# A third Strassen level inside one product of seven, with its PSUM bank held over three steps

## The chip, the cores and the metric

The kernel runs on one core of a Trainium2 chip. The metric is the device time of one launch in microseconds (us). Three timed runs of the kernel before gave 819.54, 820.01 and 820.28 us; the median is 820.01 us.

## The reference, cut to what matters

All data are fp32. `x` has 4 x 1024 tokens of 1024 features.

```
xn = layernorm(x)
g  = sigmoid(xn @ gate_w.T + gate_b);   u_g = xn * g          # gate product
s  = recurrence over tokens of b * u_g ... + d_eff * u_g      # y of the recurrent branch
h  = silu(xn @ w1.T)                                          # product "u"
h  = silu(h @ w3.T)                                           # product "m"
h  = h @ w2.T
out[expert of token] += gate of token * h                     # 8 rows receive anything (top 2 of 8)
result = x + s * silu(out)
```

Only eight rows of the routed sum are not zero, so the kernel sums the 4096 rows of `h` into eight by their gates first and multiplies by `w2` afterwards, and of the recurrence and of the gate product it computes only what these eight rows and the mean over tokens need. What is left as heavy work is the product with `w1` (called u), that with `w3` (called m), both for all 4096 tokens, and the gate product (called g) for 1024 of them.

## The kernel before

**Tiling.** The tokens are taken in four blocks of 1024, `sb` = 0 to 3. They are called groups 0 to 3 in the name of the change; here they are called blocks, because "group" is needed for something smaller. In each block the 1024x1024x1024 product u, and then m, is computed by two levels of Strassen's algorithm in Winograd's form. The outer level replaces eight 512-wide products by seven, here called groups, with the indices 1 to 7. The order in which they run is written in the dictionary `order` (L205): 1, 2, 5, 6, 7, 4, 3 for u and 1, 5, 6, 2, 7, 4, 3 for m. The inner level replaces the eight 256-wide products of a group by seven, here called small products. `small` (L869) issues one: four matmuls of 128x128 weights with 256 moving columns, which sum into one PSUM bank of 128x512. An operand of a group is a `block` (128x4x512, four quadrants of 128x512), and a sum of quadrants is a `quarter` (128x512). There are 20 blocks and 18 quarters (L125), both handed out in a ring: `Held` (L111) pops the one that was dropped longest ago.

**One group.** `Half.step(n)` (L919) runs the seven small products of a group, n = 0 to 6, into three banks: X for n = 0, 2, 4, 6; Z for n = 1, 5; Y for n = 3. X and Z come from pools of two banks, Y from a pool of one (L104 to 106). After each product VectorE (DVE) adds the bank to a quadrant of the result: `first` for the first product that reaches a quadrant, `more` for a later one. Where there is nothing to add yet (groups 1 and 5), `first` is a copy by ScalarE (ACT). `whole` (L1005) follows when a quadrant is complete: in groups 6 and 7 it is one more DVE addition of two blocks for each quadrant, and in the groups that finish a block of results it calls `done`, where ACT applies the SiLU in place. The product of n = 3 is the one that the change replaces:

```python
            elif n == 3:
                Y = ps_y.tile([P, 2 * Q], F32, tag="Y", name=f"Y_{self.tag}")
                go(Y, A[:, 1], t[:, 2], True, True)
                ...
                    self.more(0, Y)
```

**Order.** Every engine runs its instructions in the order in which the program is written (`Pinned`, L79). That order is made by places. One place is the time of one small product; a group starts seven places after the one before it, and its step n stands at place S + 2n, S being its start. So the steps of two neighbouring groups alternate: between step 3 of one group at S + 6 and step 4 at S + 8 lies step 0 of the next group at S + 7. Everything else is put at a place with `at` (L186), and is issued by `run_todo` ahead of the step that stands there. A generator gives up its turn with `yield`, and goes on that many places later.

**What stands around the steps.** `left_sums` (L846) makes the four sums of token quadrants of a group on GpSimd (POOL), from place S - 6 on. The sums of weight quadrants are made in block 0 (`fresh_sums`, L546), stored in HBM, and loaded again in blocks 1 to 3 by the queue of SyncE (SP): `load_kept` and `load_kept_sum` (L629, L635). `s1` to `s4` (L785 to L844) make the four sums of token blocks of the outer level, on POOL for u of blocks 1 to 3 and on DVE elsewhere. `norm` (L407) normalises the tokens of the next block on DVE during m. `route` (L439) finds the experts of a block early in its u: TensorE computes the logits, DVE finds the two largest and their indices, ACT takes the sigmoids of their difference, and DVE builds the gates (tiles `lg`, `mx`, `ix`, `df`, `oh`, `C`). `scatter` (L1060) sums the finished rows of a block into eight.

Of the kernel before, what the change touches and what calls it, by code (L numbers as in the profile page):

```python
# [10 lines left out]
F32 = mybir.dt.float32  # L11
# [3 lines left out]
ALU = mybir.AluOpType  # L15
AX = mybir.AxisListType
P = 128
Q = 256
# [4 lines left out]
def kernel(  # L23
# [49 lines left out]
    NS = NTOK // SB  # L73
# [5 lines left out]
    class Pinned:  # L79
# [15 lines left out]
    nc = tc.nc  # L95
    pe, dve, act, pool, sync = (
        Pinned(e) for e in (nc.tensor, nc.vector, nc.scalar, nc.gpsimd, nc.sync)
    )
# [7 lines left out]
    ps_y = ctx.enter_context(tc.tile_pool(name="ps_y", bufs=1, space=bass.MemoryType.PSUM))  # L106
# [15 lines left out]
            if self.uses == 0:  # L122
                self.home.append(self.tile)

    NB, NQ = 20, 18  # L125
    IDLE = 13
    blocks = deque(
        const.tile([P, 4, 2 * Q], F32, tag=f"b{i}", name=f"b{i}") for i in range(NB)
# [8 lines left out]
    def quarter(uses=1):  # L137
        return Held(quarters, uses)
# [47 lines left out]
    def at(place, f, *args):  # L186

        seq[0] += 1
        heapq.heappush(todo, (place, seq[0], f, args))
# [8 lines left out]
    def resume(p, g):  # L198
        step = next(g, None)
        if step is not None:  # L200
            at(p + step, resume, p + step, g)
# [14 lines left out]
    start = {}  # L216
# [301 lines left out]
    kept = {}  # L518
    op_t = {}
# [14 lines left out]
    def keep_quarter(name, i, j, o):  # L534
        d = dramp.tile([P, 2 * Q], F32, tag=f"{name}_{i}_{j}", name=f"{name}_{i}_{j}")
        sync.dma_start(d, o.tile)
        kept[name, i, j] = d
        o.drop()
# [177 lines left out]
    def first_w3():  # L716
# [48 lines left out]
    S_OF = {  # L765
        1: (0, 0),
        2: (0, 1),
        4: (1, 1),
        5: "s1",
        6: "s2",  # L770
        3: "s4",
        7: "s3",
    }
    left = {}
# [91 lines left out]
                yield 2 * (A_AT[j + 1] - A_AT[j])  # L866


    def small(ps, A, B, start, stop, rows_first):  # L869

        for mt in range(2):
            for kt in range(2):
                w, m = (A, B) if rows_first else (B, A)
                pe.matmul(
                    ps[:, mt * Q : (mt + 1) * Q],
                    w[:, kt * Q + mt * P : kt * Q + (mt + 1) * P],
                    m[:, kt * Q : (kt + 1) * Q],
                    start=(start and mt == 0 and kt == 0),
                    stop=(stop and mt == 1 and kt == 1),
                    skip_group_check=True,  # L880
                )
# [3 lines left out]
    class Half:  # L885
# [30 lines left out]
        def whole(self, q):  # L916
            whole(self.kind, self.sb, self.i, q)

        def step(self, n):  # L919
            if n == 0:  # L920
                self.begin()
            A, t = self.A, self.t
            ts = [op_ts.get((self.kind, self.sb, self.i, j)) for j in range(4)]
            s = [left_q.get((self.src, self.sb, self.i, j)) for j in range(4)]

            def go(ps, a, b, start, stop):
                small(ps, a, b, start, stop, self.rows_first)

            if self.plain:

                q = ((0, 1, 2, 3) if self.i == 1 else (0, 3, 1, 2))[n // 2]
                ps = self.X if n // 2 % 2 == 0 else self.Z
                go(ps, A[:, q // 2 * 2 + n % 2], t[:, n % 2 * 2 + q % 2], n % 2 == 0, n % 2 == 1)
                if n % 2:
                    self.first(q, ps)
            elif n == 0:
                go(self.X, A[:, 0], t[:, 0], True, False)
                self.first(0, self.X)
            elif n == 1:
                go(self.Z, s[0].tile, ts[0].tile, True, False)  # L940
                self.first(3, self.Z)
                s[0].drop()
                ts[0].drop()
            elif n == 2:
                go(self.X, s[1].tile, ts[1].tile, False, False)
                self.first(1, self.X)
                s[1].drop()
                ts[1].drop()
            elif n == 3:
                Y = ps_y.tile([P, 2 * Q], F32, tag="Y", name=f"Y_{self.tag}")  # L950
                go(Y, A[:, 1], t[:, 2], True, True)
                if (self.kind, self.i) == ("g", 1):
                    at(Y_AT, self.more, 0, Y)
                else:
                    self.more(0, Y)
            elif n == 4:
                go(self.X, s[2].tile, ts[2].tile, False, False)
                self.more(3, self.X)
                s[2].drop()
                ts[2].drop()  # L960
            elif n == 5:
                go(self.Z, s[3].tile, t[:, 3], False, True)
                self.more(1, self.Z)
                s[3].drop()
            elif n == 6:
                go(self.X, A[:, 3], ts[3].tile, False, True)
                self.first(2, self.X)
                self.whole(2)
                ts[3].drop()
            if n == (7 if self.plain else 6):  # L970
                self.A.drop()
                t.drop()
# [265 lines left out]
    for kind, sb, i, plain in line:  # L1238
        h = Half(kind, sb, i, plain)
        halves.append(h)  # L1240
        S = start[kind, sb, i]
        n = 2 if sb == 0 and kind == "u" and i not in PLAIN_G else 1
        if kind != "g" and not plain:
            at(S + 2 - 8, left_sums, kind, sb, i, n)
        if kind != "g" and sb > 0:
            at(S - 10, load_kept, kind, sb, i)
            for j in range(4):
                at(S + 2 * T_AT[j] - 9, load_kept_sum, kind, sb, i, j)

    for sb in range(NS):  # L1250
        n = 2 if sb == 0 else 1
# [252 lines left out]
```

## Time and profile before

| | us |
|---|---|
| median of three timed runs | 820.01 |
| span of the profiled execution, first to last instruction | 817.9 |
| PE (TensorE matmul) busy | 810.6, 99% of the span |
| PEld (weight loads) busy | 696.5 |
| DVE busy | 509.7 |
| POOL busy | 496.1 |
| ACT busy | 263.8 |

The page gives no other time for the profiled execution than its span; the median of the timed runs lies 2.1 us above it. A row of the profile names the line, the engine, the operation, "out<-in" by the names of the tiles without their numbers, the shapes and the count. One fp32 matmul shows as two records on PE and two weight loads on PEld, so a small product is eight records. All work goes through the helper at L89, so rows are told apart by the names of the tiles. In the rows of the timeline the columns are the start, the time from the first start to the last end, the engine and its work, and, in brackets, how long the engine stood idle before it and who ended that. The ends of matmuls are modelled: a record of 0.38 us overlaps the next one, which starts 0.216 us after it.

By stretches of the span, u of blocks 1, 2 and 3 runs at about 290 to 375, 460 to 545 and 630 to 712 us, and m of block 3 from 712 to the end. POOL is busy for 52.6 us of the 85 us from 290 to 375.

### The profile page before, as it was taken

How to read it: one execution, taken by the hardware profiler on the slowest of the kernel's cores; microseconds unless marked ns; L12 is line 12 of the kernel's file. 1: busy time of each engine (PE TensorE's matmuls, PEld its weight loads, DVE VectorE, ACT ScalarE, POOL GpSimd, SP SyncE). 2: the span in 40 equal slices, each digit the busy share in tenths (PEclk: the TensorE clock that was granted, in tenths of full speed). 3: DMA queues.
4: the chain of work that ended last, by engine and by line, in shares of the span. 5: the costliest groups of instructions: out<-in, count | busy, mean ns of one | idle time of the engine just before them, and what ended most of it. 6: DMA issues, size and time to landing. Idle time of an engine off the chain costs nothing.

```text
span 817.9 us, 11299 instructions
## 1 busy us (share of the span) xinstructions
PE 810.6 (99%) x4085; PEld 696.5 (85%) x4085; DVE 509.7 (62%) x868; ACT 263.8 (32%) x458; POOL 496.1 (61%) x398
## 2 busy tenths in 40 slices
PE   8999999999999999999999999999999999999997
PEld 7888888888888878888888788888888788888885
DVE  6886598765588524764985235666983246667643
ACT  1245126877232237341022065421122021220111
POOL 2799896967999394744547453755448454465300
PEclk9999999999999999999999999999999999999999
DMA  9946619465978947629955875559666365555700
GB/s 338 421 175 232 230 47 357 171 246 160 411 267 309 345 174 293 241 103 385 376 179 210 332 279 190 187 206 426 242 244 257 104 219 203 196 180 195 283 14 2
DMA packets 55927, 192.88 MB, mean 236 GB/s; under 512 B 6480, under 2 KB 9792, under 8 KB 44224
## 3 DMA queue, kind: packets, MB, share of 16 engines
q1 hardware_dynamic: 55552, 191.61, 63.5%
q8 instruction: 33, 0.54, 0.3%
q10 hardware_dynamic: 320, 0.54, 0.2%
q14 instruction: 22, 0.18, 0.1%
HBM read 169.01 MB, written 39.87 MB: 255 GB/s over the span
## 4 chain that ended last, share of the span: by engine, by line
PE 98%; DMA 1%; DVE 0%; ACT 0%; issue 0%; SPq 0%
PE X_u L89 24%; PE X_m L89 24%; PE Z_u L89 12%; PE Z_m L89 12%; PE X_g L89 6%; PE Y_m L89 6%; PE Y_u L89 6%; PE Z_g L89 3%; PE acc L89 2%; PE plT L89 2%; PE Y_g L89 1%; DMA b<-in_x 1%; PE pp L89 0%; DVE bn L89 0%; PE accB L89 0%; PE ta L89 0%
## 5 line engine op out<-in xcount | busy, mean ns | idle before, releaser
L89 POOL TENSOR_TENSOR q<-b 128x512 f32<-128x512 f32 x154 | 203.0, 1331 | 193.7 <-PE X_m L89 48.0
L89 ACT ACTIVATE b<-b 128x512 f32<-128x512 f32 (+1 forms) x152 | 105.3, 696 | 298.1 <-DVE b L89 291.6
L89 POOL TENSOR_TENSOR q<-b,q 128x512 f32<-128x512 f32 x98 | 133.1, 1361 | 7.2 <-issue 4.0
L89 POOL TENSOR_TENSOR b<-b,b 128x512 f32<-128x512 f32 x72 | 92.9, 1310 | 48.5 <-PE X_u L89 33.7
L89 DVE TENSOR_TENSOR b<-b,b 128x512 f32<-128x512 f32 x120 | 109.2, 925 | 2.7
L89 PE MATMUL X_m<-q,q 128*128 128x256 f32 x448 | 105.9, 379 | 0.0
L89 PE MATMUL X_u<-q,q 128*128 128x256 f32 x432 | 102.4, 380 | 0.0
L89 DVE TENSOR_TENSOR b<-X_u,b 128x512 f32<-128x512 f32 x87 | 60.0, 690 | 57.8 <-PE X_u L89 57.1
L89 DVE TENSOR_TENSOR b<-X_m,b 128x512 f32<-128x512 f32 x88 | 60.4, 688 | 56.9 <-PE X_m L89 56.7
L89 PEld LDWEIGHTS X_m<-q,q 128*128 128x128 f32 x448 | 85.0, 190 | 12.4 <-issue 0.8
L89 POOL TENSOR_TENSOR q<-q,b 128x512 f32<-128x512 f32 x56 | 73.6, 1314 | 32.4 <-PE X_u L89 25.1
L89 PEld LDWEIGHTS X_u<-q,q 128*128 128x128 f32 x432 | 81.8, 190 | 12.2 <-issue 1.2
L89 DVE TENSOR_TENSOR b<-b,bc 128x1024 f32<-128x1024 f32 x56 | 67.8, 1211 | 0.1
L89 PE MATMUL X_u<-b,b 128*128 128x256 f32 x248 | 58.4, 380 | 0.0
L89 PE MATMUL Y_m<-b,b 128*128 128x256 f32 x224 | 53.1, 380 | 0.0
L89 PE MATMUL Z_m<-b,q 128*128 128x256 f32 x224 | 53.0, 380 | 0.0
L89 PE MATMUL X_m<-b,b 128*128 128x256 f32 x224 | 53.0, 379 | 0.0
L89 PE MATMUL Z_m<-q,q 128*128 128x256 f32 x224 | 52.9, 379 | 0.0
L89 PE MATMUL X_m<-q,b 128*128 128x256 f32 x224 | 52.9, 379 | 0.0
L89 PEld LDWEIGHTS X_u<-b,b 128*128 128x128 f32 x248 | 47.0, 190 | 6.7 <-DVE b L89 0.4
L89 DVE TENSOR_TENSOR b<-Z_u,b 128x512 f32<-128x512 f32 x47 | 32.4, 690 | 31.6 <-PE Z_u L89 30.7
L89 PE MATMUL Z_u<-q,q 128*128 128x256 f32 x216 | 51.1, 380 | 0.0
(182 smaller groups left out, 1171.6 us busy)
## 6 DMA issues: line engine op xcount, KB each, us to landing
q<-w SPq DMA_DIRECT2D x168, 256.0 KB, 4.5
b<-in_w SPq DMA_DIRECT2D x36, 1024.0 KB, 9.0
b<-w_T SPq DMA_DIRECT2D x24, 1024.0 KB, 6.3
b<-in_xT SPq DMA_DIRECT2D x15, 1024.0 KB, 12.9
w<-q SPq DMA_DIRECT2D x56, 256.0 KB, 7.4
b<-in_x SPq DMA_DIRECT2D x12, 1024.0 KB, 11.0
w_T<-b SPq DMA_DIRECT2D x8, 1024.0 KB, 4.4
b<-in_gw SPq DMA_DIRECT2D x6, 1024.0 KB, 14.0
```

The source lines that it names most:

```text
L89: r = f(*args, **kwargs)
```

## The change

In u of blocks 1 to 3 and in m of block 3, 28 groups in all, the small product of step 3 is computed by a third level of Strassen's algorithm: seven products of 128x128x128, each one matmul with 128 moving columns, in place of eight (that is, of four matmuls with 256). All go into bank Y of the group, which is now taken at the first of three steps:

- `eighth(0)` at place S + 1: two matmuls, and two DVE additions of 128x128 from the bank to the result;
- `eighth(1)` at place S + 3.6: one matmul and one such addition, of a quarter of the bank that is summed on;
- `eighth(2)` in step 3 at S + 6: four matmuls, one DVE addition of the whole bank (128x512), and one of 128x128.

The operands of the third level are sums of quarters of a quadrant. `token_thirds` makes three on POOL for each of the 28 groups at S - 2; `weight_thirds` makes four on POOL at S - 3, for u of block 1 and m of block 3; in u of block 1 they are stored in HBM, and `load_thirds` loads them at S - 3 in u of blocks 2 and 3. The ring of quarters grows from 18 to 24, and the argument `dynamic_dma_scratch_size=1024` makes room for it.

```diff
-    NB, NQ = 20, 18
+    NB, NQ = 20, 24
...
+    def is_third(kind, sb, i):
+        return sb > 0 and kind == "u" or (kind, sb) == ("m", NS - 1)
+    def cut(t):
+        return t.rearrange("p (k n) -> p k n", n=P)
+    def token_thirds(kind, sb, i):
+        a = cut(left[kind, sb, S_OF[i]][:, 1])
+        t = quarter()
+        o = cut(t.tile)
+        third_s[kind, sb, i] = t
+        pool.tensor_tensor(
+            o[:, 0:2], a[:, 1:2].to_broadcast([P, 2, P]), a[:, 0::3], ALU.subtract
+        )
+        yield 1
+        pool.tensor_tensor(o[:, 2], a[:, 0], o[:, 1], ALU.subtract)
+        pool.tensor_tensor(o[:, 3], a[:, 2], o[:, 2], ALU.subtract)
+    def weight_thirds(kind, sb, i):
...
+        pool.tensor_tensor(o[:, 1], b[:, 1], b[:, 0], ALU.subtract)
+        yield 1
+        pool.tensor_tensor(o[:, 2], b[:, 3], o[:, 1], ALU.add)
+        pool.tensor_tensor(o[:, 3], b[:, 2], o[:, 2], ALU.subtract)
+        yield 1
+        pool.tensor_tensor(o[:, 0], b[:, 1], b[:, 3], ALU.add)
+        yield 1
+        if again:
+            keep_quarter(name, i, "t", t)
+    def load_thirds(kind, sb, i):
+        o = quarter()
+        sync.dma_start(o.tile, kept[{"u": "w1", "m": "w3"}[kind], i, "t"])
+        third_t[kind, sb, i] = o
...
+        def eighth(self, n):
...
+            d = cut(self.dst[:, 0])
+            z, w = (1, 2) if self.rows_first else (2, 1)
+            if n == 0:
+                self.Y = ps_y.tile([P, 2 * Q], F32, tag="Y", name=f"Y_{self.tag}")
+            ps = cut(self.Y)
...
+            if n == 0:
+                go(3, a[:, 0], b[:, 0], True, False)
+                go(z, S[:, 1], T[:, 1], False, False)
+                add(d[:, 0], ps[:, 3])
+                add(d[:, 3], ps[:, z])
+            elif n == 1:
+                go(3, S[:, 2], T[:, 2], False, False)
+                add(d[:, z], ps[:, 3])
+            else:
+                go(z, S[:, 3], b[:, 3], False, False)
+                go(w, a[:, 3], T[:, 3], False, False)
+                go(0, a[:, 2], b[:, 2], False, False)
+                go(3, S[:, 0], T[:, 0], False, True)
+                add(self.dst[:, 0], self.Y)
+                add(d[:, w], ps[:, 3])
+                third_s[key].drop()
+                third_t[key].drop()
+                self.whole(0)
...
+            elif n == 3 and is_third(self.kind, self.sb, self.i):
+                self.eighth(2)
...
+        if is_third(kind, sb, i):
+            for n, step in enumerate((1, 3.6)):
+                at(S + step, h.eighth, n)
+            at(S - 2, token_thirds, kind, sb, i)
+            fresh = sb == 1 or kind == "m"
+            at(S - 3, weight_thirds if fresh else load_thirds, kind, sb, i)
```

## Prediction

> **What bounds the kernel now.** I read the page first: the busy time by engine and the chain that ended last.
>
> ```profile
> PE 810.6 (99%) x4085; PEld 696.5 (85%) x4085; DVE 509.7 (62%) x868; ACT 263.8 (32%) x458; POOL 496.1 (61%) x398
> ...
> PE 98%; DMA 1%; DVE 0%; ACT 0%; issue 0%; SPq 0%
> ```
>
> PE is busy all the time and carries the chain; in the waits by engine PE has none after 9 us of more than 0.3 us. So PE time that is taken away is gained, if no wait takes its place. Both sides need short times, so I went on to the timeline: what a record with 128 columns costs, and how long PE's banks take to come back.
>
> ```profile
> 8.75 0.83 PE L89 MATMUL idle<-ident,ones 128*128 128x128 f32 x6
> ...
> 805.20 0.60 PE L89 MATMUL tT<-ident,b 128*128 128x128 f32 x4
> 805.64 1.89 PE L89 MATMUL X_m<-q,b 128*128 128x256 f32 x8
> ```
>
> In a row of n records the spacing is (time - one record)/(n - 1). With 256 columns it is (1.89 - 0.38)/7 = 0.216 us. With 128 columns and full weights it is (0.83 - 0.276)/5 = 0.111 in `idle` and (0.60 - 0.272)/3 = 0.109 in the transposes `tT`, which have other weights each time. I take `idle`, which is a true fp32 matmul of two records.
>
> **The gain.** A small product is 8 x 0.216 = 1.73 us now, and 14 x 0.111 = 1.55 in three pieces of 0.44, 0.22 and 0.89. That is 0.17 us for each of 28, or 4.9 us (5.7 by `tT`, 2.1 by the 0.118 of `ta`, which is bound by its loads).
>
> A rule speaks against that. The Trainium skill, "TensorE: Matmul & The Clock Gate", Part 3, "The mechanism", says that a weight load overlaps a running matmul only where the two use different row groups. By it a record would wait for its own load, at least 0.109 more by `ta`, and the change would cost 28 x (14 x 0.22 - 1.73) = 38 us. The 0.111 of `idle` with a load for each record does not agree with it, and I go by the row.
>
> **The price: less cover for the banks.** Now every bank is followed by whole products of 1.73 us before PE needs it, or its neighbour, again. These rows show how long a bank takes to come back.
>
> ```profile
> 34.53 0.65 DVE L89 TENSOR_TENSOR b<-X_g,b 128x512 f32<-128x512 f32 x1
> 35.23 0.94 PEld L89 LDWEIGHTS X_g<-b,q 128*128 128x128 f32 x5 [0.35 <-DVE b L89]
> 35.23 1.13 PE L89 MATMUL X_g<-b,q 128*128 128x256 f32 x4
> ```
>
> DVE ends at 35.18 and PE goes on 0.05 later. The load isn't hidden then: the first record takes 0.48 in place of 0.38, so 0.10 more. In front of it, DVE starts 0.20 us after the next product's first record (X_u below: Y_u's first at 485.17, the addition at 485.37), because the last record drains. An addition takes 0.69, or 0.72 if the next one needs its result (756.37 - 755.65 on DVE); a 128x128 one I put at 0.29, from 0.42 for 256 and 0.69 for 512 columns.
>
> *Bank X.* Step 0 of the next group, at S + 7, takes the bank that the group before read out after its step 6, at S + 5. What lies between is step 3, now 0.89 instead of 1.73. The bank needs 0.20 + 0.69 + 0.05 + 0.10 = 1.05 (1.04 unrounded): 0.16 late. Where ACT copies (groups 1 and 5: 0.19 + 0.585 + 0.15 = 0.93) it is 0.04. In each of four stretches of seven groups it is five of the first kind and two of the second: 20 x 0.16 + 8 x 0.04 = 3.5 us. Bounds: 0, if release and load are quicker by 0.16, and 4.5.
>
> *Bank Y.* It is one bank only. So far seven places lie between two uses; now `eighth(2)` ends at S + 7 and the next group's `eighth(0)` stands at S + 8, one product later. It needs 0.20 + 0.72 + 0.29 + 0.05 + 0.10 = 1.36, and has 0.16 (from X) + 1.73 = 1.89. So an ordinary group costs nothing, but every delay on DVE over 0.5 us stops PE. I looked for such delays.
>
> First, `route`:
>
> ```profile
> 485.17 1.89 PE L89 MATMUL Y_u<-b,b 128*128 128x256 f32 x8
> 486.90 1.89 PE L89 MATMUL X_u<-b,b 128*128 128x256 f32 x8
> ...
> 485.37 0.69 DVE L89 TENSOR_TENSOR b<-X_u,b 128x512 f32<-128x512 f32 x1 [0.50 <-PE X_u L89]
> 488.46 0.23 DVE L89 TENSOR_TENSOR oh<-pl,ix 128x64 f32<-128x64 f32 x1 [2.40 <-ACT pl L89]
> 488.60 0.68 DVE L89 TENSOR_TENSOR b<-Y_u,b 128x512 f32<-128x512 f32 x1
> ...
> 486.09 0.63 ACT L89 ACTIVATE b<-b 128x512 f32<-128x512 f32 x1 [0.91 <-DVE b L89]
> 486.74 1.28 ACT L89 ACT_TABLE_LOAD   x1
> 488.04 0.39 ACT L89 ACTIVATE pl<-df 128x8 f32<-128x8 f32 x2
> ```
>
> DVE's `oh` waits 2.40 us for ACT, which has a SiLU and a 1.28 us table load ahead of the sigmoids. The addition of Y_u queues behind `oh` and starts at 488.60, 1.54 after Y_u has ended. Today nobody waits for that. In the changed program the order on DVE is the same: X_u, `oh`, then the two additions of `eighth(2)`; the next group's first matmul in Y waits for them. All of ACT's chain starts with the X_u addition at 485.37, which does not move. PE then reaches that matmul at 485.17 + 0.89 + 0.16 + 1.73 = 487.95; the bank is there at 488.60 + 0.72 + 0.29 + 0.15 = 489.76. That is 1.8 us, and `oh` waits the same 2.40 in all three blocks: 5.4 us (bounds 4 and 6.6, by 0.4 us to either side).
>
> Second, the extra additions of `whole`, and `s1` and `s4` of the last m:
>
> ```profile
> 509.54 0.69 DVE L89 TENSOR_TENSOR b<-X_u,b 128x512 f32<-128x512 f32 x1 [1.03 <-PE X_u L89]
> 510.34 1.06 DVE L89 TENSOR_TENSOR b<-b,b 128x512 f32<-128x512 f32 x1
> 511.32 0.68 DVE L89 TENSOR_TENSOR b<-Y_u,b 128x512 f32<-128x512 f32 x1
> ...
> 711.14 1.28 DVE L89 TENSOR_TENSOR b<-b,b 128x512 f32<-128x512 f32 x2
> 712.06 1.89 PE L89 MATMUL X_m<-b,b 128*128 128x256 f32 x8
> 712.34 0.68 DVE L89 TENSOR_TENSOR b<-Y_u,b 128x512 f32<-128x512 f32 x1
> ```
>
> After group 6 of u the last `whole` (1.06) stands before the Y addition. PE: 509.34 + 0.89 + 0.16 + 1.73 = 512.12; bank: 511.32 + 1.16 = 512.48; 0.36, three times: 1.1 us. After group 7 that addition takes 0.71 and costs nothing. Such b<-b,b rows run from 0.67 to 1.80, longest beside POOL, so the bounds over six places are 0 and 6. At the end of block 3's u, two sums of `s1` come first: PE is ready at 710.33 + 2.78 = 713.11, the bank at 712.34 + 1.16 = 713.50: 0.4. At `s4` (757.4 to 764.0) DVE works without a gap; the Y_m product starts at 759.57, its addition at 761.82, 0.2 later with `eighth(1)` ahead: 763.2 against 762.35, 0.85. Together 1.25 (0 to 2.5).
>
> **What I cost at nothing.** POOL gets 140 instructions. Its 128x512 sum takes 1.27 us alone; a MEMSET takes 0.205 for 128 and 0.31 for 256 columns, so a 128x128 sum lies between 0.32 (a quarter) and 1.27; I take 0.4, as sizes count in MEMSET, and 0.7 for 128x256. The seven groups of u in block 1 get 7 x (0.7 + 2 x 0.4 + 4 x 0.4) = 22 us on top of 52.6 busy of 85: it fits, and the work runs ahead by the ring. Without that cover (all at 1.27: 62 us) POOL would be 30 us late there. SP gets seven stores and fourteen loads of 256 KB, which pass the queue's later loads; such a load lands in 4.5 us, and from S - 3 to S + 1 there are 6.9; if a load came late, its first matmul would stop for the difference, 0 to 2 us each. The larger ring only renames and leads further. The scratch argument concerns no queue with traffic on the page: 0. The other new DVE additions, 3 x 0.29 in a group, lie in gaps.
>
> **The sum.** -4.9 + 3.5 + 5.4 + 1.1 + 1.25 = +6.4. On the profiled execution: 817.9 + 6.4 = 824.3; the median lies 2.1 above the span, so 820.0 + 6.4 = 826.4. A measurement of this kernel can tell about 0.2%, 1.6 us, from no change.
>
> **Rivals.**
> - *PE's gain stays, the waits don't come* (0.11): the bank is back in time, because the addition overlaps more than I think, or ACT's sigmoids come earlier. Then 820.0 - 4.9 = 815.1. It speaks for it that PE has never waited for DVE so far; against it, that the order on DVE puts `oh` ahead and 1.73 us of cover can't hold 2.4. It decides in favour of faster if the waits sum to less than 3.3 us.
> - *POOL and its port* (0.08): the small sums cost nearer to 1.27, or slow DVE's b<-b,b rows to 1.75 at all eight places (8 x 0.7 more). 832 or more.
> - *The third level saves PE nothing* (0.04), if mixed 128-column loads are not hidden as in `idle`: up to 858.
> - *About balanced* (0.05): X costs nothing and `route` 1.3 a time: 0 + 3.9 + 0.5 - 4.9, 819.5 to 821.5.
>
> My own case has 0.72 and a range of 822 to 831 by its bounds. Range for all: 821.5 to 832. Chances: faster 0.11, within 0.2% 0.06, slower 0.83.
>
> **What would show it.** Right: PE busy some 5 us less in its records and new idle of PE, over 10 us, in front of Y and X "<-DVE b"; three single waits near 1.6 to 1.8 us, one in each u of blocks 1 to 3, where DVE waits for ACT at `oh`; many of about 0.1 to 0.2 at X_u and X_m; Y rows of 128 columns 0.11 us apart. Wrong: no idle on PE, Y records 0.2 apart, or PE waiting for POOL or DMA.

## The result, and the profile after

The changed kernel takes 830.95 us (median of four runs, 830.59 to 831.16) against 819.99 us, a ratio of 1.0133 with a 95% interval of 1.0119 to 1.0148. It is slower by 11.0 us, where 826.4 was forecast with a range of 821.5 to 832. The profiled execution spans 828.8 us, 10.9 more than the one before.

The page, the lines that answer to those shown of the kernel before:

```profile
PE 812.7 (98%) x4253; PEld 699.0 (84%) x4253; DVE 538.7 (65%) x980; ACT 263.5 (32%) x458; POOL 568.9 (69%) x538
...
PE 90%; DVE 5%; DMA 3%; ACT 1%; issue 0%; SPq 0%; DVEq 0%
```

PE has 168 records more, as 28 products went from 8 to 14, and yet is hardly busier (812.7 against 810.6). The new thing is in the chain: DVE has 5% of it, where it had 0%. (DMA has 3% for 1%, but PE's list below names no wait for a DMA, and the kernel with the second Y bank, below, has the same 3% at 819 us.) The waits by engine, PE's own, say where (columns: who waited for whom, us in total, times, the longest):

```profile
PE Y_u L89 <- DVE oh L89: 4.9, 3, 1.6
PE Y_u L89 <- DVE b L89: 2.3, 6, 0.8
PE Y_m L89 <- DVE b L89: 1.8, 3, 1.3
```

Before the change the list had no wait of PE in these stretches. Now twelve stand in front of bank Y. The list holds idle time only and is too small in two ways. The weight load behind a wait is no longer hidden, which costs 0.10 us more for 256 columns and 0.07 for 128 and counts as busy; and short waits are not listed. So I took the starts of PE's records from 270 to 806 us and counted what lies above the regular spacing of 0.216 us (256 columns) or 0.111 (128):

| where PE loses time, us | forecast | after |
|---|---|---|
| Y behind `oh`, 3 times | 5.4 | 5.6 |
| Y after group 6 of u, 3 times | 1.1 | 1.3 |
| Y after group 7 of u, in blocks 2 and 3 | 0 | 2.0 |
| Y in m of block 3 and at its start | 1.25 | 2.7 |
| Y at the second group of block 1 | not listed | 0.4 |
| X at the start of the next group | 3.5 | 3.1 |
| together | 11.3 | 15.1 |
| gain of the shorter product | -4.9 | -4.7 |
| sum | +6.4 | +10.4 |

Of the remaining 0.5 us to the 10.9 of the spans, 0.3 lie in the first 30 us, ahead of every changed group (PE's first work on `bc` starts at 29.76 in place of 29.47; in the other runs between 29.4 and 31.0), and 0.2 behind PE's last record. The gain is 28 x (8 x 0.216 - 14 x 0.1115): the Y records of 128 columns start 0.109 to 0.112 us apart wherever nothing is late.

The largest entry, in the timeline of PE, DVE and ACT in u of block 2 (columns as before):

```profile
489.08 0.39 PE L89 MATMUL Y_u<-q,q 128*128 128x128 f32 x2
489.36 1.99 PE L89 MATMUL X_u<-b,b 128*128 128x256 f32 x8
493.00 0.46 PE L89 MATMUL Y_u<-b,b 128*128 128x128 f32 x2 [1.64 <-DVE oh L89]
...
488.61 0.69 DVE L89 TENSOR_TENSOR b<-X_u,b 128x512 f32<-128x512 f32 x1 [0.73 <-PE X_u L89]
491.70 0.23 DVE L89 TENSOR_TENSOR oh<-pl,ix 128x64 f32<-128x64 f32 x1 [2.40 <-ACT pl L89]
491.85 1.01 DVE L89 TENSOR_TENSOR b<-Y_u,b 128x512 f32<-128x512 f32 x2
...
489.99 1.28 ACT L89 ACT_TABLE_LOAD   x1
491.28 0.39 ACT L89 ACTIVATE pl<-df 128x8 f32<-128x8 f32 x2
```

`eighth(2)` ends on PE at about 489.3; its bank could be read from 489.5 on. But DVE stands at `oh` until 491.70, because ACT loads a table and then makes the sigmoids. The two Y additions end at 492.86, and PE goes on at 493.00, after a wait of 1.64 as listed, and 1.81 by the spacing of the records. The chain from X_u to `oh` has kept its length: 2.40 us of DVE idle before and after. What changed is that somebody now waits for what stands behind it. The same lines show the X wait: `X_u` x8 takes 1.99 in place of 1.89, as its first load is exposed, and starts at 489.36, not 489.30.

### The profile page after: what moved, and what is told of

It reads as the page before. It is cut to its first block, busy times and chain, and to the rows that moved or that the text cites. A ratio compares the mean times of both kernels' runs of the same rounds, so it can differ in the third digit from the quotient of the medians.

```text
span 828.8 us, 12011 instructions
## 1 busy us (share of the span) xinstructions
PE 812.7 (98%) x4253; PEld 699.0 (84%) x4253; DVE 538.7 (65%) x980; ACT 263.5 (32%) x458; POOL 568.9 (69%) x538
## 4 chain that ended last, share of the span: by engine, by line
PE 90%; DVE 5%; DMA 3%; ACT 1%; issue 0%; SPq 0%; DVEq 0%
PE X_m L89 22%; PE X_u L89 21%; PE Z_m L89 12%; PE Z_u L89 11%; PE Y_m L89 6%; PE X_g L89 5%; DVE b L89 5%; PE Y_u L89 4%; PE Z_g L89 3%; PE acc L89 2%; PE plT L89 2%; DMA b<-in_xT 2%; DMA b<-in_x 1%; PE Y_g L89 1%; ACT L89 0%
## 5 line engine op out<-in xcount | busy, mean ns | idle before, releaser
L89 POOL TENSOR_TENSOR q<-b 128x512 f32<-128x512 f32 (+2 forms) x210 | 238.6, 1151 | 135.4 <-DVE b L89 50.4
L89 POOL TENSOR_TENSOR q<-b,q 128x128 f32<-128x128 f32 (+1 forms) x182 | 173.0, 955 | 12.4 <-PE X_u L89 7.2
L89 PEld LDWEIGHTS X_u<-q,q 128*128 128x128 f32 x432 | 78.9, 190 | 10.3 <-issue 1.2
L89 POOL TENSOR_TENSOR q<-q,b 128x512 f32<-128x512 f32 x56 | 75.4, 1346 | 12.6 <-PE X_m L89 9.9
L89 DVE TENSOR_TENSOR b<-Y_u,b 128x128 f32<-128x128 f32 (+1 forms) x111 | 40.7, 383 | 25.9 <-PE Y_u L89 17.2
L89 DVE TENSOR_TENSOR b<-Z_m,b 128x512 f32<-128x512 f32 x48 | 32.6, 686 | 30.0 <-PE Z_m L89 29.7
```

Source lines behind the costliest of these rows:

```text
L89: r = f(*args, **kwargs)
```

## The experiments

Two theories were set against each other. By the first, the matmuls save what they should, and the loss is the release of PSUM banks: Y, held from S + 1 to S + 6, is wanted again one product later, and X has 0.89 us of cover in place of 1.73. By the rival, POOL's 140 sums, the transfers and what POOL's work does to DVE's (the expectations call this the port) slow the kernel, whatever the banks do. The expectations put the waits at X at 2.9 us: they leave out four delays of 0.05 that are in the 3.1 of the table. The first four runs undo one thing each, and shared one chip; the kernel before took 819.32 there. The later runs were on other chips, so a gain over the changed kernel is given below as the difference of the two distances from the kernel before on the same chip; the changed kernel lies 11.0 us above it. The 95% intervals leave about 0.8 to 1.4 us to either side of each distance.

**A second Y bank.**

```diff
-                self.Y = ps_y.tile([P, 2 * Q], F32, tag="Y", name=f"Y_{self.tag}")
+                if order[self.kind].index(self.i) % 2:
+                    self.Y = ps_acc.tile([P, 2 * Q], F32, tag="rows", name=f"Y_{self.tag}")
+                else:
+                    self.Y = ps_y.tile([P, 2 * Q], F32, tag="Y", name=f"Y_{self.tag}")
```

> The changed kernel, but every second third-level group takes its bank from a second one (the bank of the `rows` tiles, which stands idle in these stretches). Theory (release of the one Y bank): in the trace of the changed kernel PE stands still for 12.0 us in front of Y and for 2.9 us in front of X. With a second bank the Y part goes, X stays and may grow to 3.5 where a Y wait had covered it: 831.0 - 12.0 + 0.5 = 819.5 us (818.5 to 820.5). Rival (POOL's 140 sums and the port that they share with DVE slow everything): the sums are all still there, so 829 us or more. Rival (matmuls of 128 columns are dearer than 0.111 us a record): nothing changes, 831 us.

Measured: 819.13 us, ratio 0.9994 (0.9984 to 1.0003), no difference from the kernel before. All work of the change is still in it, POOL is as busy as in the changed kernel (569.1 us), and of the 12.0 us in front of Y 0.7 are left, counted as in the table. In the waits of PE in this kernel one line is left of the three:

```profile
PE Y_m L89 <- DVE b L89: 0.2, 1, 0.2
```

**One place later.**

```diff
-            for n, step in enumerate((1, 3.6)):
+            for n, step in enumerate((2, 3.6)):
```

> The changed kernel, but `eighth(0)` stands one place later (S + 2 in place of S + 1), still with one Y bank. Theory: one more product of 1.73 us lies between the last use of the bank by one group and the first by the next, so only what is over 1.73 of each wait is left: about 0.15 in each of three blocks behind `oh`, the rest goes. 831.0 - 12.0 + 0.5 + 0.5 = 820.0 us (819 to 821). Rival (POOL and port): the work is the same, 829 us or more. If a second bank helps and this does not, it is not the time of release but something else about the bank.

Measured: 819.62 us, ratio 1.0000 (0.9991 to 1.0010). With one bank, too, 10.6 of the 12.0 us go when the next group asks for it 1.73 us later. The timeline of PE at the place shown above:

```profile
486.11 1.99 PE L89 MATMUL X_u<-b,b 128*128 128x256 f32 x8
487.94 1.89 PE L89 MATMUL X_u<-q,q 128*128 128x256 f32 x8
490.05 0.46 PE L89 MATMUL Y_u<-b,b 128*128 128x128 f32 x2 [0.22 <-DVE b L89]
```

Two products stand between the uses of the bank now, and 0.22 us of idle is left of 1.64. So it is the time of release against the time of the next use that counts; nothing else about the bank is needed to explain the loss.

**`route` one place later.**

```diff
         dve.tensor_sub(df, mx[:, :, 0], mx1)
-        yield 1
+        yield 2 if sb else 1
```

> The changed kernel, but in blocks 1 to 3 `route` goes on one place later after `df`, so that `oh`, which waits for ACT, stands behind the two additions of `eighth(2)` in DVE's order and not ahead of them. Theory: the three waits of 1.81 + 0.07 us behind `oh` go, nothing else changes: 831.0 - 5.6 = 825.4 us (824.5 to 826.5). Rival (the waits at `oh` are only where a general lateness of DVE shows): the time stays within 1 us of 831, and the waits turn up at other places.

Measured: 824.77 us, ratio 1.0065 (1.0048 to 1.0081): 5.5 us above the kernel before in place of 11.0, so 5.5 us gained, 5.6 expected. The timeline of DVE shows the two instructions exchanged:

```profile
487.52 1.02 DVE L89 TENSOR_TENSOR b<-Y_u,b 128x512 f32<-128x512 f32 x2 [0.20 <-PE Y_u L89]
490.76 0.22 DVE L89 TENSOR_TENSOR oh<-pl,ix 128x64 f32<-128x64 f32 x1 [2.22 <-ACT pl L89]
```

`oh` still waits 2.22 us for ACT, but behind the Y additions, and the wait costs PE nothing. In PE's waits the line of `oh` is gone, and the two others stand unchanged (2.3 and 1.8).

**The sums alone.**

```diff
             elif n == 3 and is_third(self.kind, self.sb, self.i):
-                self.eighth(2)
+                Y = ps_y.tile([P, 2 * Q], F32, tag="Y", name=f"Y_{self.tag}")
+                go(Y, A[:, 1], t[:, 2], True, True)
+                self.more(0, Y)
...
-            for n, step in enumerate((1, 3.6)):
-                at(S + step, h.eighth, n)
```

> The changed kernel with all its new sums on POOL, their stores and loads, and the ring of 24 quarters, but with the product of step 3 as before (256 columns, one step, the third level's sums not used). Theory: POOL, SP and port cost nothing by themselves: 820.0 us (819.2 to 821.0). Rival (POOL and port): most of the 11 us stays, 826 us or more.

Measured: 819.63 us, ratio 1.0002 (0.9993 to 1.0012), with POOL at 568.5 us. The rival falls in its plain form: the sums, stores and loads cost nothing while nobody's bank depends on DVE being on time.

**Where the forecast was short: the additions of `whole`.** In u the additions of groups 6 and 7 stand on DVE ahead of the Y additions. This edit gives them one operand in PSUM:

```diff
-            if k == ("m", 0):
+            if k == ("m", 0) or kind == "u" and sb > 0:
...
-        yield from spare_bank((0, 2))
+        yield from spare_bank((0, 2) if not scattered else (1,))
```

> The changed kernel, but in u of blocks 1 to 3 the additions of `whole` in groups 6 and 7 take one operand from PSUM (ACT copies it there first, into the idle `rows` bank), so that DVE doesn't read two operands from SBUF. Theory: the Y waits after groups 6 and 7 (three of 0.36 and two of 0.93 us, each with 0.07 more) come from these additions being held up by POOL's sums, 1.06 to 1.75 us in place of 0.69: they go, 831.0 - 3.3 = 827.7 us (827 to 828.7). Rival (DVE is late there by the number of its instructions, which stays): 830.5 us or more.

Measured: 827.71 us against 819.84, ratio 1.0097 (1.0082 to 1.0113): 7.9 us above in place of 11.0, so 3.1 us gained, 3.3 expected. The timelines of DVE and of POOL in the changed kernel, and then in this one:

```profile
527.07 0.69 DVE L89 TENSOR_TENSOR b<-X_u,b 128x512 f32<-128x512 f32 x1 [1.03 <-PE X_u L89]
527.79 1.75 DVE L89 TENSOR_TENSOR b<-b,b 128x512 f32<-128x512 f32 x1
529.47 1.00 DVE L89 TENSOR_TENSOR b<-Y_u,b 128x512 f32<-128x512 f32 x2
...
527.73 2.94 POOL L89 TENSOR_TENSOR q<-b 128x512 f32<-128x512 f32 x2
```

```profile
526.47 0.69 DVE L89 TENSOR_TENSOR b<-X_u,b 128x512 f32<-128x512 f32 x1 [1.04 <-PE X_u L89]
527.26 0.69 DVE L89 TENSOR_TENSOR b<-b,spare 128x512 f32<-128x512 f32 x1
527.87 1.01 DVE L89 TENSOR_TENSOR b<-Y_u,b 128x512 f32<-128x512 f32 x2
...
525.72 2.51 POOL L89 TENSOR_TENSOR q<-b 128x512 f32<-128x512 f32 x2
```

POOL's sum began 0.06 us ahead of DVE's addition of two SBUF operands, and that took 1.75 us. With an operand in PSUM it takes 0.69, though the second of POOL's sums runs through it; the Y additions follow 1.40 after X_u in place of 2.40, and of PE's waits after groups 6 and 7 less than 0.06 us each is left. The meeting is not quite the same, but after group 6 it is, with a sum of POOL that began 0.75 us ahead. The changed kernel, and then this one:

```profile
336.53 1.06 DVE L89 TENSOR_TENSOR b<-b,b 128x512 f32<-128x512 f32 x1
335.78 1.27 POOL L89 TENSOR_TENSOR b<-b,b 128x512 f32<-128x512 f32 x1 [7.11 <-PE X_u L89]
...
336.65 0.69 DVE L89 TENSOR_TENSOR b<-b,spare 128x512 f32<-128x512 f32 x1
335.90 1.27 POOL L89 TENSOR_TENSOR b<-b,b 128x512 f32<-128x512 f32 x1 [7.62 <-PE X_u L89]
```

The addition takes 1.06 us with two SBUF operands and 0.69 with one in PSUM. So POOL does have a part, not by its load as a whole but where one of its sums starts just ahead of a DVE addition that a bank waits behind. In the kernel with the sums alone DVE is busy for 512.4 us against 509.7 before the change, and it costs nothing, since nobody waits.

**Waits at X.** In the next three runs steps 5 and 6 of the groups change places, so that X is read out two places earlier (and `done` fires on the quadrant that is then last):

```diff
-            elif n == 5:
+            elif n == (6 if is_swapped(self.kind, self.sb, self.i) else 5):
                 go(self.Z, s[3].tile, t[:, 3], False, True)
...
-            elif n == 6:
+            elif n == (5 if is_swapped(self.kind, self.sb, self.i) else 6):
                 go(self.X, A[:, 3], ts[3].tile, False, True)
```

What they change in the computation: the next group's `first(1)` reads a quadrant of the result one place before the exchanged step has added to it, so one term is missing in it. The instructions and their number are the same, so the times can be read.

> The changed kernel (one Y bank, `eighth(0)` at S + 1), but steps 5 and 6 of the third-level groups change places (and of the last group of m in blocks 0 to 2), so that bank X is read out two places earlier. Theory: the 2.9 us of waits at X go, but where a Y wait follows, the X wait was part of its cover and the Y wait grows by as much; 13 of the 28 groups have one. So only about 1 us is gained: 830 us (829 to 831). Rival (waits at X and Y add up independently): 831.0 - 2.9 = 828 us.

Measured: 828.46 us against 819.84, ratio 1.0108 (1.0093 to 1.0124): 8.6 us above in place of 11.0, so 2.3 us gained. That is outside the range of the theory, though by less than the interval, and nearer to the 2.9 of the rival than to its 1: the sum was missed. No X wait is left in the stretches. The three waits behind `oh` grew from 1.81 to 1.97, by the 0.16 that X no longer gives them, as expected; but the one after group 7 in blocks 2 and 3 shrank from about 0.93 to 0.17, since DVE's addition there happened to take 0.79 us beside POOL, not 1.75, and in block 1 a new one of 0.66 came. Counted as in the table, the waits at Y together went from 12.0 to 13.3 us, where 0.16 more at each of the 13 would have added 2.1; by this count 1.8 us are gained. So the theory of the banks holds for the three fixed waits, and the sum was missed by meetings with POOL, which went both ways.

The next two add `eighth(0)` at S + 2 to this edit, and the second of them the second Y bank as well.

> `eighth(0)` one place later (S + 2), and steps 5 and 6 exchanged as in the swap alone. Theory: with Y out of the way the X waits are pure loss, so here the exchange brings its whole 2.9 us: 819.6 - 2.9 = 816.7 us (816.0 to 817.7), faster than the kernel before by 0.3 to 0.4%. Rival (the third level saves nothing on PE, the rest is waits given back): 819 to 820 us as before the change.

Measured: 816.90 us against 819.84, ratio 0.9967 (0.9955 to 0.9979). The run with one place later lies 0.3 us above the kernel before on its chip and this one 2.9 below, so with Y out of the way the exchange brings 3.2 us, 2.9 expected.

> Second Y bank, `eighth(0)` at S + 2, and steps 5 and 6 exchanged: no wait at Y or X should be left. Theory: 819.3 - 4.85 + about 1 us that the sums at the ends of stretches leave = 815.5 us (814.7 to 816.5). Rival (third level saves nothing): 819 to 820 us.

Measured: 816.29 us, ratio 0.9959 (0.9945 to 0.9972), 0.8 above the expected 815.5 but within its range. The profiled execution spans 813.9 us, 4.0 less than that of the kernel before, with one Y wait of 0.7 left, at the DVE instructions of `recurrence`. That is the gain of the third level, nearly whole.

**Versions that are faster.** The exchange breaks an order between groups, so I looked for another way to give X time: the `rows` bank, idle there, as a third bank for X.

```diff
-            self.X = ps_x.tile([P, 2 * Q], F32, tag="X", name=f"X_{self.tag}")
+            if is_third(kind, sb, i) and order[kind].index(i) in (2, 5):
+                self.X = ps_acc.tile([P, 2 * Q], F32, tag="rows", name=f"X_{self.tag}")
+            else:
+                self.X = ps_x.tile([P, 2 * Q], F32, tag="X", name=f"X_{self.tag}")
...
-            for n, step in enumerate((1, 3.6)):
+            for n, step in enumerate((2, 3.6)):
```

> `eighth(0)` at S + 2 with one Y bank, and the idle `rows` bank as a third bank for X (the third and the sixth group of each third-level stretch take it), so that a bank of X comes back one group later. No step changes its order, so every addition reads what it should. Theory: the 2.9 us of X waits go but for one at each start of a stretch, about 0.7 in all; 0.9 of Y waits stay as in the run with one place later: 819.6 - 2.2 = 817.4 us (816.6 to 818.2), 0.2 to 0.4% faster than before the change. Rival (what the exchanged steps gained came from reading too early, not from X): 819 to 820 us.

Measured: 818.56 us against 819.80, ratio 0.9983 (0.9974 to 0.9992). Faster than the kernel before, by less than forecast and outside the range: the X waits are gone but for one at the start of each stretch of u, but the Y waits behind `oh` went up, to 0.38, 0.61 and 0.31, as the X waits had been part of their cover. No step reads too early here, so what is gained does not come from that.

With `route` one place later too:

> As the run with the third X bank, and `route` one place later after `df` as well. Theory: the Y waits left behind `oh` (0.16 to 0.45 in each of three blocks) go too: 816.8 us (816.0 to 817.8). Rival as there: 819 to 820 us.

Measured: 817.14 us against 819.80, ratio 0.9965 (0.9952 to 0.9979), 2.7 us faster than the kernel before and 13.6 faster than the changed one. Of PE's waits behind DVE in the stretches the list has one:

```profile
PE Y_m L89 <- DVE b L89: 0.6, 1, 0.6
```

It stands at `recurrence` in the last m, which I did not move.

## Why the prediction was right, and where its sum was short

*The gain* was right: 4.7 us for 4.9. The rule of the Trainium skill that was weighed there, "TensorE: Matmul & The Clock Gate", Part 3, "The mechanism", would have the weight loads wait for the matmuls. The same section also lets a load go ahead of a running matmul when it targets a background weight buffer, which the prediction left out; whether that is what happens here no run shows. The Y records with a new load each, 0.109 to 0.112 us apart, do not agree with the rule: of 298 such spacings from 270 to 806 us only 15 are longer, 0.184 to 0.214, thirteen of them behind a wait and two behind other small matmuls. The run with the second Y bank, S + 2 and the exchange shows the gain in the time: 4.0 us less span, with 0.8 us of Y waits left.

*`route`* was right in mechanism, place and size: three times 1.88 for 1.8, and moving `oh` took away 5.5 us for 5.4.

*Bank X* was right in size, 3.1 for 3.5, in 17 delays of 0.16 to 0.23 and four of 0.05 (the forecast's sum of 1.05 should read 1.04). The forecast also counted the 0.16 as cover for Y, and the swap alone and the third X bank bear it out: without the X wait the waits behind `oh` grow by about as much.

*The step that was too small* is the second part of bank Y, the additions of `whole`, with `s1` and `s4`: 6.0 us after groups 6 and 7 and in the last m for the 2.35 forecast. After group 7 the forecast took the addition of 0.71 us from the trace of before and concluded "costs nothing". But that duration belongs to the moment, not to the instruction: in blocks 2 and 3 of the changed kernel it took 1.75 and 1.71. With the sums alone it took 0.95 and 0.94 there, as a short new sum began 0.05 us ahead, and the same with the second Y bank; so the new sums moved the meetings, and the times shifted by the waits at Y made them worse. The bounds (0 and 6 for groups 6 and 7, 0 to 2.5 for `s1` and `s4`) held what was listed, 3.3 and 2.0; the values did not. This is the mechanism of the rival "POOL and its port" at two of its eight places. That POOL's cost was put at nothing was right for the work and wrong for the meetings. In the last m, `s4` cost 1.5 us for 0.85, its three additions in a row taking 2.70 where they took 1.89; that these too were held up by POOL was not tested by itself. And a Y wait of 0.6 at `recurrence` and one of 0.4 behind `norm` in block 1 were not listed: the forecast looked for delays in `route`, `whole` and `s1` to `s4` only.

*The range.* The loss was forecast as 6.4 us and measured as 11.0, and 830.95 lies at the edge of the 822 to 831 that the forecast gave its own case. The bounds of its terms in fact add up to 819 to 835 (the lower bound for `route` is 4.2, not 4), so that it still fell inside the narrower range owes something to luck.

*The signs.* The three waits at `oh`, the many short ones at X and the spacing of the Y records came as described. PE's records, though, are busy for 2.1 us more, not 5 less, because some 6 of the 15.1 us lost show as longer records and not as idle time; with nearly all waits gone (second Y bank, S + 2 and exchange) they are busy for 806.7 us, 3.9 less than before. And the listed idle time is 9.0 us, not over 10, all of it in front of Y.

*Cost at nothing:* POOL, SP, ring and scratch argument by themselves cost nothing that can be measured, as the sums alone show (0.3 us). POOL's 128x128 sums took 0.51 us on average, where 0.4 was taken. The stretches given ahead of the prediction are too late at their start: in the kernel before, u of blocks 1 to 3 runs at 266 to 369, 443 to 546 and 620 to 722 us. POOL is busy for 53.6 of the 91 us from 270 to 361, so the sum made for it changes little.

## What to carry to other kernels

A product that is made shorter also takes cover from the banks around it. Before it is split over more steps, put next to each bank the time from its last write to its next use, and what the reading engine has to do in between, waits included. A wait of the reading engine that costs nothing today (2.40 us at `oh`) becomes the bound when a single bank is reused inside it. Here moving the first use by one product (10.7 us) or the waiting instruction behind the bank's reader (5.5 us) brought more than the 4.7 us that the shorter product saves.

## What the runs showed of the hardware that I had not expected

The length of DVE's addition of two SBUF operands depends on how much is left of a sum that POOL has begun: the same instruction of the same group took 0.69, 0.79 and 1.75 us in different blocks and runs, and 0.69 with one operand in PSUM. With 0.24, 0.52 and 1.21 us left of POOL's sum the addition became 0.10, 0.37 and 1.06 us longer, each time some 0.15 less than was left. And a bank that comes even a little late costs PE up to 0.10 us more than its lateness, because the weight load behind it is exposed; 0.06 us of lateness at X became 0.16, thirteen times in one execution.
